# Another order of the three engine queues in the attention part of a graph-layer kernel

## The chip, the cores and the metric

The kernel runs on one core of one Trainium2 chip. The metric is the device time of one execution in microseconds; the number given for a kernel is the median of its runs. Five engines work side by side, each through its own queue in the order in which its instructions were issued: TensorE (PE in the profile; PEld are its weight loads), VectorE (DVE), ScalarE (ACT), GpSimd (POOL) and SyncE (SP), which issues most of the transfers.

## The reference

A chain of four pre-normed layers on x (512 nodes by 512 features), with 16384 edges. Only the first, an attention layer, is touched by the change:

```python
h = jnp.maximum(_layernorm(x, axis=-1), 0.0)
q = (h @ Wq + bq).reshape(N, H, HEAD)        # 8 heads of 64
k = (h @ Wk + bk).reshape(N, H, HEAD)
v = (h @ Wv + bv).reshape(N, H, HEAD)
scores = jnp.einsum('nhd,mhd->nhm', q, k) / np.sqrt(HEAD)
adj = jnp.zeros((N, N)).at[src, dst].set(1.0)
scores = jnp.where(adj[:, None, :] == 0, -1000000000.0, scores)
attn = jax.nn.softmax(scores, axis=1)        # over the heads
attn_out = jnp.einsum('nhm,mhd->nhd', attn, v).reshape(N, D_OUT) @ Wo + bo
h1 = _layer_norm(h + attn_out, g1, be1)
ff = jax.nn.relu(h1 @ W1 + b1) @ W2 + b2
x = x + _layer_norm(h1 + ff, g2, be2)
```

After it come a neighbour mean, a mixture of four graph experts and a graph convolution, each after its own norm and ReLU of x. They use the matrix of edge counts (C and its transpose CT in the code), its row sums (cnt, pdeg) and their reciprocals.

## The kernel before, in words

The work has four stages in time. Up to about 51 us the edge counts are summed in PSUM by one-hot products (`count`, L279), with the first projections between them. From 51 to 138 us the softmax part runs. Up to 191 us follow the output projection and the feed-forward layer of the attention block. All after it, the other three layers, is the same in both kernels.

The softmax part goes over eight blocks i of 256 by 128 scores for eight heads: the columns' half hf = i // 4 (LEFT or RIGHT) and the row block b = i % 4. For each block, in this chain:

- `scores(i)` (L310, PE): eight small products into one tile psc of four PSUM banks. There is one such tile, so the next block's scores wait until this one is read for the last time.
- `copies(i)` (L321, ACT): the scores as bf16. `maximum(i)` (L326 to 328, DVE): three steps down to the maximum over the heads. `maximum_far(i)` (L334, DVE): adds a large number where there is no edge.
- `minus_max(i)`: on PE as a product (L348), or for i of 0, 5 and 7 on DVE (L344). `exponent(i)` (L354, ACT).
- off that chain: `total(i)` (L363 to 366, DVE) the sum, `logs(i)` (L373, 374, ACT) and `weight(i)` (L380, 381, DVE) its reciprocal, `spread(i)` (L386, DVE) the scaling, `gather(i)` (L396, PE) the product with v into aps, `squares(i)` (L357, ACT) a check value.

Between these steps lie others: `v_mm` and `v_add` (L403, L407) make v, `project_mm` and `project_out` (L201, L243) the right half of q, `digits` (L502 to 510, DVE) and the call that it returns, `dg[b]()` (L511, ACT) make the counts CT, `add_bo` (L410, DVE) adds a bias to h.

The part after it: `heads_out` (L414, ACT) moves aps into qT; `wo_mm` (L418, PE) is the output projection; `residual` (L422, DVE), `stats_begin`, `stats_end` and `norm1` are the first norm; `turn1` (L439, PE) and `turn1_out` (L444, ACT) transpose it; `ff_up_mm` (L201 into pff, PE) and `ff_up_out` (L465, ACT) the first feed-forward product in four pairs f = 0, 2, 4, 6 per half; `ff_down` (L474, PE) the second, one product pd per row block; `affine1` (L449, 450) and `add_be2` (L492) are DVE steps that prepare the residuals; `norm2_a` (L480), `norm2_b` (L485, and statistics of the new x) and `norm2_c` (L185, ACT, the scaled h) are the second norm and the next layer's first. `turn(hT, h, b, "h2_")` (L196 PE, L197 ACT) transposes that h. `count_turn(b)` (L428, PE) transposes the counts, and the call that it returns, `ct[b]()` (L429, ACT), writes C. `score_check`, `check_mm` (L520, PE: a product of one row, pall) and `check_out` (L525, DVE) make one flag. `pdeg` is a product with ones that sums C, and the lines from L804 on its reciprocals and others, on DVE.

With `ff_down(3)` the part ends. Its residual on DVE (y23), the norms of row block 3 and its transpose must be done before the next layer's sums of hT (`ws_hT`, L866) and with them the product pbe_b (L900).

What sets the order: the block is written under a manual schedule of PE, DVE and ACT. Each engine executes its instructions in the order in which the calls stand in the source, and waits at each for its inputs and for its output buffer. PSUM tiles come from small pools: `banks[:] = [(ps_mm, "mm")]` names the pool that the next `bank()` draws from. ps_mm has two buffers and ps_x four; ps_x takes the room of psc, once the last block is through. Weight loads are issued by SP in their own order, each once the last reader of the buffer that it takes is done:

```python
wpool = ctx.enter_context(tc.tile_pool(name="wpool", bufs=5))
ps_mm = tc.alloc_tile_pool(name="ps_mm", bufs=2, space=PSUM)
ps_sc = tc.alloc_tile_pool(name="ps_sc", bufs=1, space=PSUM)
```

Of the kernel before, what the change touches and what calls it, by code (L numbers as in the profile page):

```python
# [27 lines left out]
FB = FF // P  # L28
# [10 lines left out]
def fast(  # L39
# [4 lines left out]
    nc = tc.nc  # L44
# [279 lines left out]
    def maximum(i):  # L324
        a, b = high[i]
        nc.vector.tensor_tensor(a, a, b, op=ALU.max)  # L326
        nc.vector.tensor_tensor(a[:, 0:2, :], a[:, 0:2, :], a[:, 2:4, :], op=ALU.max)
        nc.vector.tensor_tensor(a[:, 0, :], a[:, 0, :], a[:, 1, :], op=ALU.max)
        high[i] = a[:, 0, :]

    def maximum_far(i):
        hf, b, cols = place(i)
        far[i] = soft.tile([P, W], R, tag="mr", name=f"mr{i}")
        nc.vector.tensor_add(far[i], high[i], none[:, b, cols])  # L334
# [117 lines left out]
    ffT = {}  # L452

    def ff_up_mm(hf, f):

        if f == 0:
            ffT[hf] = ffp.tile([P, FB, W], F32, tag="ffT", name=f"ffT{hf}")
        p = bank(f"pff{hf}_{f}").rearrange("p (i n) -> p i n", i=2)
        for i in range(2):
            mm(p[:, i, :], [(blk(w1[f // 4], k, (f + i) % 4), hT[:, k, hf * W:(hf + 1) * W]) for k in range(KB)])  # L460
        return p
# [67 lines left out]
    with tc.manual_schedule(engines={ET.PE, ET.DVE, ET.Activation}):  # L529
# [58 lines left out]
        vi = soft.tile([P, M], I32, tag="vi", bufs=1, name="vi")  # L588
        banks[:] = [(ps_mm, "mm")]
        pj, pv, dg, ct, pw, ys, st, rs, tp, pu, pd, y2, a2, n1 = ({} for _ in range(14))  # L590
        maximum(0)
        pv[0] = v_mm(0)
        nc.vector.tensor_copy(vi, cps)
        dg[0] = digits(0)
        maximum_far(0)
        minus_max(0)
        v_add(0, pv[0])
        squares(0)
        dg[1] = digits(1)
        exponent(0)  # L600
        scores(1)
        total(0)
        copies(1)
        maximum(1)
        maximum_far(1)
        dg[0]()
        add_bo(2)
        dg[3] = digits(3)
        dg[2] = digits(2)
        logs(0)  # L610
        pv[1] = v_mm(1)
        v_add(1, pv[1])
        minus_max(1)
        exponent(1)
        pj[2] = project_mm(wq, BQ, 2, RIGHT)
        weight(0)
        scores(2)
        spread(0)
        squares(1)
        project_out(pj[2], qT, BQ, 2, RIGHT)  # L620
        copies(2)
        pj[0] = project_mm(wq, BQ, 0, RIGHT)
        maximum(2)
        maximum_far(2)
        pj[1] = project_mm(wq, BQ, 1, RIGHT)
        total(1)
# [7 lines left out]
        project_out(pj[0], qT, BQ, 0, RIGHT)
        project_out(pj[1], qT, BQ, 1, RIGHT)
        scores(3)
        logs(1)
        weight(1)
        pj[3] = project_mm(wq, BQ, 3, RIGHT)
        copies(3)  # L640
        spread(1)
        maximum(3)
        maximum_far(3)
        pv[2] = v_mm(2)
        minus_max(3)
        logs(2)
        gather(1)
        project_out(pj[3], qT, BQ, 3, RIGHT)
        squares(3)
        weight(2)  # L650
        exponent(3)
        add_bo(0)
        dg[2]()
        dg[1]()
        spread(2)
        v_add(2, pv[2])
        total(3)
        scores(4)
        copies(4)
        pv[3] = v_mm(3)  # L660
        maximum(4)
        logs(3)
        maximum_far(4)
        squares(4)
        add_bo(1)
        v_add(3, pv[3])
        weight(3)
        minus_max(4)
        exponent(4)
        gather(2)  # L670
        scores(5)
        spread(3)
        total(4)
        copies(5)
        gather(3)
        maximum(5)
        ct[1] = count_turn(1)
        heads_out(0)
        maximum_far(5)
        pw[0] = bank("pwo0")  # L680
        wo_mm(0, pw[0], range(KB))
        logs(4)
        minus_max(5)
        squares(5)
        weight(4)
        ct[1]()
        scores(6)
        copies(6)
        pw[1] = bank("pwo1")
        wo_mm(1, pw[1], range(KB))  # L690
        spread(4)
        ys[0] = residual(pw[0], 0, "y")
        st[0] = stats_begin([ys[0]], "l1_0")
        exponent(5)
        ct[0] = count_turn(0)
        maximum(6)
        rs[0] = stats_end(st[0])
        ct[0]()
        ys[1] = residual(pw[1], 1, "y")
        st[1] = stats_begin([ys[1]], "l1_1")  # L700
        maximum_far(6)
        norm1(0, ys[0], *rs[0])
        rs[1] = stats_end(st[1])
        norm1(1, ys[1], *rs[1])
        squares(6)
        gather(4)
        minus_max(6)
        tp[0] = turn1(0)
        total(5)
        exponent(6)  # L710
        turn1_out(0, tp[0])
        scores(7)
        logs(5)
        pu[0, 0] = ff_up_mm(0, 0)
        total(6)
        copies(7)
        pu[0, 2] = ff_up_mm(0, 2)
        ff_up_out(0, 0, pu[0, 0])
        weight(5)
        maximum(7)  # L720
        maximum_far(7)
        logs(6)
        minus_max(7)
        spread(5)
        pu[0, 4] = ff_up_mm(0, 4)
        exponent(7)
        gather(5)
        total(7)
        logs(7)
        weight(6)  # L730
        spread(6)
        ps_sc.release()
        ps_x = tc.alloc_tile_pool(name="ps_x", bufs=4, space=PSUM, reuse_waits="tile")
        banks[:] = [(ps_x, "x")]
        pu[0, 6] = ff_up_mm(0, 6)
        weight(7)
        gather(6)
        spread(7)
        nc.vector.tensor_add(be1_b, be1_b, b2_b)
        affine1(1)  # L740
        gather(7)
        squares(7)
        banks[:] = [(ps_mm, "mm")]
        score_check()
        pall = check_mm()
        check_out(pall)
        ff_up_out(0, 4, pu[0, 4])
        heads_out(1)
        ff_up_out(0, 2, pu[0, 2])
        banks[:] = [(ps_x, "x")]  # L750
        pw[3] = bank("pwo3")
        wo_mm(3, pw[3], range(KB))
        add_be2(1)
        pw[2] = bank("pwo2")
        wo_mm(2, pw[2], range(KB))
        ff_up_out(0, 6, pu[0, 6])
        ys[3] = residual(pw[3], 3, "y")
        st[3] = stats_begin([ys[3]], "l1_3")
        rs[3] = stats_end(st[3])
        norm1(3, ys[3], *rs[3])  # L760
        ys[2] = residual(pw[2], 2, "y")
        st[2] = stats_begin([ys[2]], "l1_2")
        affine1(0)
        rs[2] = stats_end(st[2])
        add_be2(0)
        norm1(2, ys[2], *rs[2])
        pd[1] = bank("pf21")
        ff_down(1, pd[1], range(FB))
        y2[1] = residual(pd[1], 1, "y2")
        banks[:] = [(ps_mm, "mm")]  # L770
        tp[1] = turn1(1)
        turn1_out(1, tp[1])
        a2[1] = norm2_a(1, y2[1])
        affine1(2)
        banks[:] = [(ps_x, "x")]
        pd[0] = bank("pf20")
        ff_down(0, pd[0], range(FB))
        pu[1, 4] = ff_up_mm(1, 4)
        banks[:] = [(ps_mm, "mm")]
        ct[2] = count_turn(2)  # L780
        n1[1] = norm2_b(1, *a2[1])
        affine1(3)
        norm2_c(1, n1[1])
        y2[0] = residual(pd[0], 0, "y2")
        a2[0] = norm2_a(0, y2[0])
        banks[:] = [(ps_x, "x")]
        pu[1, 6] = ff_up_mm(1, 6)
        pu[1, 2] = ff_up_mm(1, 2)
        pu[1, 0] = ff_up_mm(1, 0)
        ff_up_out(1, 4, pu[1, 4])  # L790
        n1[0] = norm2_b(0, *a2[0])
        ff_up_out(1, 2, pu[1, 2])
        banks[:] = [(ps_mm, "mm")]
        ct[3] = count_turn(3)
        add_be2(3)
        ff_up_out(1, 6, pu[1, 6])
        add_be2(2)
        ct[2]()
        ff_up_out(1, 0, pu[1, 0])
        norm2_c(0, n1[0])  # L800
        ct[3]()
# [4 lines left out]
        nc.vector.reciprocal(ideg_b, ideg_b)
        ideg = const.tile([P, NB], F32, name="ideg")
        icnt = const.tile([P, NB], F32, name="icnt")
# [9 lines left out]
        nc.vector.reciprocal(icnt, icnt)  # L818
        nc.vector.reciprocal(nanf, cnt)
        nc.vector.tensor_scalar(nanf, nanf, 0.0, None, op0=ALU.mult)  # L820
        banks[:] = [(ps_mm, "mm")]
        turn(hT, h, 0, "h2_")
        turn(hT, h, 1, "h2_")
        banks[:] = [(ps_x, "x")]
        p2, p3 = bank("pf22"), bank("pf23")
        ff_down(2, p2, range(FB))
        y = residual(p2, 2, "y2")
        n1 = norm2_b(2, *norm2_a(2, y))
        norm2_c(2, n1)
        ff_down(3, p3, range(FB))  # L830
        y23 = residual(p3, 3, "y2")
# [875 lines left out]
```

## Time and profile before

| | us |
|---|---|
| median of 3 runs | 500.74 (498.92 to 501.13) |
| time of the profiled execution | 498.76 |
| span of the profiled execution | 496.9 |
| mean granted TensorE clock in it | 0.997 |
| TensorE busy, 51 to 116 us (65.00) | 59.15 |
| TensorE busy, 116 to 138 us (22.00) | 21.83 |
| TensorE busy, 138 to 191 us (53.00) | 51.67 |
| TensorE busy, 191 to 203 us (12.00) | 11.60 |
| TensorE busy, 203 to 230 us (27.00) | 26.25 |

How to read it: times within the profile count from the start of its span. A row of the timeline has the start, the time, the engine, the line, the operation, output and inputs, and in brackets how long the engine had been idle before it and what ended that. A row of the chain has start, time and what; the chain is followed back from the last instruction, at each step to what released it. A row of the waits has the total, the number and the longest wait. Matmul rows include the end of the pipeline, so that the next can start a little before one ends. Busy TensorE is not TensorE at its peak.

### The profile page before, as it was taken

Reading aid. Unit: us, or ns where it says so; the run is one execution under the profiler, and the core shown is the slowest. Engines: PE = TensorE matmul, PEld = TensorE weight load, DVE = VectorE, ACT = ScalarE, POOL = GpSimd, SP = SyncE. Lnnn points to the kernel's source line nnn. Section 1 sums busy time; section 2 is a strip of 40 time slices with the busy share of each in tenths; the row PEclk is TensorE's granted clock in tenths of the full one; section 3 lists DMA queues with packets and bytes.
Section 4 is the critical chain, followed back from the end, with each engine's and each line's share of the span. In section 5 each row is a group of like instructions: output and inputs, shape, how many; then the busy total and the mean of one; then the engine's idle time right before and its main releaser. Section 6 shows DMA issues by size and latency. Waiting matters only on the chain.

```text
span 496.9 us, 5670 instructions
## 1 busy us (share of the span) xinstructions
PE 470.6 (95%) x2140; PEld 355.2 (71%) x2140; DVE 347.5 (70%) x752; ACT 173.1 (35%) x352; POOL 2.8 (1%) x10
## 2 busy tenths in 40 slices
PE   2999899998999989999999999999999999999995
PEld 1888465547745845677888888888888888885643
DVE  8998989899968457889857169713784147646842
ACT  3899557657222322216011121203102111122443
POOL 2000000000000000000000000000000000000000
PEclk9999999999999999999999999999999999999998
DMA  7820202300031325050004042204121040000002
GB/s 265 288 95 1 85 1 84 128 0 2 0 92 43 121 86 190 0 168 3 1 0 169 7 163 86 84 1 160 22 89 69 1 169 1 1 1 0 0 1 90
DMA packets 18498, 34.42 MB, mean 69 GB/s; under 512 B 1528, under 2 KB 2080, under 8 KB 18464
## 3 DMA queue, kind: packets, MB, share of 16 engines
q1 hardware_dynamic: 17504, 32.47, 19.3%
q10 hardware_dynamic: 960, 1.51, 0.9%
q8 instruction: 19, 0.31, 0.2%
q14 instruction: 15, 0.12, 0.1%
HBM read 32.93 MB, written 1.05 MB: 68 GB/s over the span
## 4 chain that ended last, share of the span: by engine, by line
PE 76%; DVE 15%; ACT 6%; issue 2%; DMA 0%; DVEq 0%; ACTq 0%
PE pe_b L900 8%; PE pq L201 6%; PE pe_a L900 6%; PE pf L474 6%; PE pe_c L900 5%; PE pqk L201 4%; PE pz_b L900 4%; PE po_b L900 3%; PE ph L201 3%; PE pff L201 3%; PE pal L201 3%; PE po L201 3%; PE cps L279 3%; PE pz_c L900 2%; PE po_c L900 2%; PE pz_a L900 2%
## 5 line engine op out<-in xcount | busy, mean ns | idle before, releaser
L906 DVE TENSOR_TENSOR u_sum<-pe_b,u_first 128x512 f32<-128x512 f32 x12 | 8.3, 690 | 48.8 <-PE pe_b L900 48.8
L201 PE MATMUL pq<-zz,C 128*128 128x512 f32 x128 | 32.6, 408 | 0.0
L1161 ACT ACTIVATE re<-te,gt 128x512 f32<-128x512 f32 x16 | 11.6, 723 | 55.9 <-DVE te L1159 55.9
L277 DVE TENSOR_SCALAR ohs<-iota_h,src_f,dw_i 128x256 bf16<-128x256 f16 x102 | 28.0, 342 | 2.4 <-PE cps L279 2.4
L1123 ACT ACTIVATE eT<-u_sum,vecs 128x256 f32<-128x256 f32 x24 | 10.9, 500 | 50.9 <-DVE u_sum L906 50.9
L201 PE MATMUL pff<-hT,w 128*128 128x256 f32 x128 | 28.5, 381 | 0.0
L201 PEld LDWEIGHTS pq<-zz,C 128*128 128x128 f32 x128 | 23.9, 188 | 6.4 <-issue 1.0
L474 PE MATMUL pf<-w,ffT 128*128 128x512 f32 x64 | 28.0, 592 | 0.0
L201 PEld LDWEIGHTS pff<-hT,w 128*128 128x128 f32 x128 | 24.1, 190 | 4.3 <-issue 0.6
L279 PE MATMUL cps<-ohs,ohd 128*128 128x256 bf16 x102 | 17.5, 281 | 9.6 <-DVE ohs L277 9.6
L279 PEld LDWEIGHTS <-ohd 128*128 128x128 f16 x128 | 15.2, 145 | 11.3 <-DVE ohd L268 8.5
L474 PEld LDWEIGHTS pf<-w,ffT 128*128 128x128 f32 x64 | 12.0, 190 | 14.3 <-issue 14.3
L843 ACT CAST zz<-u_sum 128x512 fp32r<-128x512 f32 x12 | 7.4, 618 | 37.7 <-DVE u_sum L906 37.7
L310 PE MATMUL psc<-qT,kT 64*128 64x256 f32 x128 | 16.0, 389 | 3.1 <-ACT s L354 1.7
L321 ACT CAST m<-psc 128x1024 bf16<-128x1024 f32 x16 | 15.4, 1014 | 9.8 <-PE psc L310 9.8
L386 DVE SCALAR_TENSOR_TENSOR s<-s,r 128x2048 f32<-128x2048 f32 x8 | 18.3, 2290 | 0.2
L310 PEld LDWEIGHTS psc<-qT,kT 64*128 64x128 f32 x128 | 12.0, 186 | 7.6 <-ACT s L354 3.7
L906 DVE TENSOR_TENSOR u_sum<-pz_b,u_first 128x512 f32<-128x512 f32 x12 | 8.3, 690 | 11.9 <-PE pz_b L900 11.6
L900 PE MATMUL pe_b<-sums,wr 128*128 128x256 f32 x64 | 16.4, 379 | 0.0
L900 PE MATMUL pe_b<-sums,wl 128*128 128x256 f32 x64 | 16.4, 379 | 0.0
L1162 DVE TENSOR_TENSOR xs<-xs,re 128x512 f32<-128x512 f32 x16 | 11.0, 690 | 7.6 <-ACT re L1161 7.6
L201 PE MATMUL pqk<-hT,wk 128*128 128x256 f32 x64 | 15.2, 381 | 0.9 <-ACT hT L197 0.9
(312 smaller groups left out, 1056.3 us busy)
## 6 DMA issues: line engine op xcount, KB each, us to landing
wr<-in_L_gnn_Wr_dram SPq DMA_DIRECT2D x8, 1024.0 KB, 5.1
wl<-in_L_gnn_Wl_dram SPq DMA_DIRECT2D x8, 1024.0 KB
w<-in_L_gnn_W_dram SPq DMA_DIRECT2D x5, 1024.0 KB, 10.6
wq<-in_L_gnn_Wq_dram ACTq DMA_DIRECT2D x1, 1024.0 KB
wk<-in_L_gnn_Wk_dram SPq DMA_DIRECT2D x1, 1024.0 KB
wv<-in_L_gnn_Wv_dram SPq DMA_DIRECT2D x1, 1024.0 KB, 5.2
wo<-in_L_gnn_Wo_dram SPq DMA_DIRECT2D x1, 1024.0 KB
bl_b<-in_L_gnn_bl_dram SPq DMA_DIRECT2D x4, 256.0 KB, 3.2
```

The source lines that it names most:

```text
L201: nc.tensor.matmul(p, a, c, start=(i == 0), stop=(i == len(pairs) - 1))
L277: nc.vector.tensor_scalar(ohs, iota_h, src_f[:, c:c + 1], dw_f[:, c:c + 1], op0=ALU.is_equal, op1=ALU.mult)
L279: nc.tensor.matmul(cps, ohd[0][:, :, c % 8], ohs, start=(c == 0), stop=(c == NCH - 1))
L310: nc.tensor.matmul(psc[i][:, 4 * g + j, :], kT[o:o + HD, j, b * P:(b + 1) * P], qT[o:o + HD, j, cols], start=(j % 2 == 0), stop=True, skip ...
L321: nc.scalar.copy(t[k].rearrange("p (g j) n -> p g j n", g=2), p[:, :, 2 * k:2 * k + 2, :])
L386: nc.vector.scalar_tensor_tensor(s, s, LEAST, rz[i].to_broadcast([P, H, W]), op0=ALU.max, op1=ALU.mult)
L474: nc.tensor.matmul(p, ffT[b // 2][:, f, c:c + P], w2[f // 4][:, f % 4, :], start=(f == 0), stop=(f == FB - 1))
L900: nc.tensor.matmul(p[:, m, :], l[i][:, k, m * P:(m + 1) * P], r[i][:, k, :], start=fresh, stop=(k == 1), skip_group_check=True)
L906: nc.vector.tensor_add(t, p, x)
L1123: nc.scalar.activation(eT[:, 2 * i + m, j * W:(j + 1) * W], v[:, m, :], AF.Relu, bias=vecs[:, o:o + 1])
L1161: nc.scalar.activation(r, t, AF.Relu, scale=gt[:, b, e:e + 1])
L1162: nc.vector.tensor_add(xs[:, b, :], xs[:, b, :], r)
```

## The change

The change puts the calls from `ohp.release()` to the third down product into another order. The calls themselves are the same, with the same shapes, and so are the kernel before and after this stretch. Three further points go with it: the tile ffT is now made at whichever pair f comes first, since the pairs come in the order 6, 2, 0, 4; the pair that is drawn from ps_x first is now f = 0; and the fourth down product gets its bank on its own. The diff, cut to the moves that the text speaks of:

```diff
-        if f == 0:
+        if hf not in ffT:
             ffT[hf] = ffp.tile([P, FB, W], F32, tag="ffT", name=f"ffT{hf}")
...
+        pv[0] = v_mm(0)
+        add_bo(1)
         maximum(0)
-        pv[0] = v_mm(0)
         nc.vector.tensor_copy(vi, cps)
...
+        total(1)
         pj[0] = project_mm(wq, BQ, 0, RIGHT)
         maximum(2)
+        project_out(pj[1], qT, BQ, 1, RIGHT)
+        logs(1)
         maximum_far(2)
-        pj[1] = project_mm(wq, BQ, 1, RIGHT)
-        total(1)
+        spread(0)
+        project_out(pj[0], qT, BQ, 0, RIGHT)
+        weight(1)
         minus_max(2)
-        add_bo(3)
+        exponent(2)
+        pj[3] = project_mm(wq, BQ, 3, RIGHT)
+        dg[2]()
+        scores(3)
         dg[3]()
-        gather(0)
-        exponent(2)
+        pv[2] = v_mm(2)
+        project_out(pj[3], qT, BQ, 3, RIGHT)
+        spread(1)
         total(2)
         squares(2)
...
         copies(3)
-        spread(1)
         maximum(3)
+        gather(0)
+        logs(2)
         maximum_far(3)
-        pv[2] = v_mm(2)
         minus_max(3)
...
         scores(5)
-        spread(3)
-        total(4)
         copies(5)
+        dg[1]()
         gather(3)
-        maximum(5)
         ct[1] = count_turn(1)
         heads_out(0)
-        maximum_far(5)
+        total(4)
         pw[0] = bank("pwo0")
         wo_mm(0, pw[0], range(KB))
+        maximum(5)
         logs(4)
+        maximum_far(5)
+        ct[1]()
         minus_max(5)
...
         rs[0] = stats_end(st[0])
-        ct[0]()
+        ct[0] = count_turn(0)
+        maximum_far(6)
+        squares(6)
         ys[1] = residual(pw[1], 1, "y")
         st[1] = stats_begin([ys[1]], "l1_1")
-        maximum_far(6)
         norm1(0, ys[0], *rs[0])
+        minus_max(6)
+        ct[0]()
         rs[1] = stats_end(st[1])
+        exponent(6)
+        gather(4)
         norm1(1, ys[1], *rs[1])
-        squares(6)
-        gather(4)
-        minus_max(6)
         tp[0] = turn1(0)
-        total(5)
-        exponent(6)
         turn1_out(0, tp[0])
         scores(7)
+        total(5)
+        total(6)
+        nc.vector.tensor_add(be1_b, be1_b, b2_b)
+        copies(7)
         logs(5)
-        pu[0, 0] = ff_up_mm(0, 0)
-        total(6)
-        copies(7)
+        maximum(7)
+        weight(5)
+        pu[0, 6] = ff_up_mm(0, 6)
+        maximum_far(7)
+        minus_max(7)
+        exponent(7)
         pu[0, 2] = ff_up_mm(0, 2)
...
+        banks[:] = [(ps_mm, "mm")]
+        ct[2] = count_turn(2)
+        affine1(0)
         squares(7)
-        banks[:] = [(ps_mm, "mm")]
+        ct[3] = count_turn(3)
+        add_be2(0)
+        heads_out(1)
         score_check()
         pall = check_mm()
         check_out(pall)
         ff_up_out(0, 4, pu[0, 4])
-        heads_out(1)
-        ff_up_out(0, 2, pu[0, 2])
+        ff_up_out(0, 0, pu[0, 0])
+        affine1(1)
+        ct[3]()
         banks[:] = [(ps_x, "x")]
         pw[3] = bank("pwo3")
         wo_mm(3, pw[3], range(KB))
...
         pd[0] = bank("pf20")
         ff_down(0, pd[0], range(FB))
+        turn1_out(1, tp[1])
+        a2[1] = norm2_a(1, y2[1])
+        y2[0] = residual(pd[0], 0, "y2")
         n1[1] = norm2_b(1, *a2[1])
         pu[1, 6] = ff_up_mm(1, 6)
         pu[1, 2] = ff_up_mm(1, 2)
+        ff_up_out(1, 6, pu[1, 6])
+        a2[0] = norm2_a(0, y2[0])
+        ff_up_out(1, 2, pu[1, 2])
+        n1[0] = norm2_b(0, *a2[0])
+        norm2_c(1, n1[1])
+        affine1(3)
+        affine1(2)
+        norm2_c(0, n1[0])
+        add_be2(2)
+        pu[1, 4] = ff_up_mm(1, 4)
+        ff_up_out(1, 4, pu[1, 4])
         pu[1, 0] = ff_up_mm(1, 0)
+        ff_up_out(1, 0, pu[1, 0])
...
         nc.vector.tensor_scalar(ideg_b, pdeg, 1.0, None, op0=ALU.max)
         banks[:] = [(ps_x, "x")]
+        turn(hT, h, 1, "h2_")
+        add_be2(3)
+        pd[2] = bank("pf22")
+        ff_down(2, pd[2], range(FB))
+        y2[2] = residual(pd[2], 2, "y2")
+        turn(hT, h, 0, "h2_")
+        a2[2] = norm2_a(2, y2[2])
+        banks[:] = [(ps_mm, "mm")]
         nc.vector.reciprocal(ideg_b, ideg_b)
...
         nc.vector.tensor_scalar(nanf, nanf, 0.0, None, op0=ALU.mult)
-        banks[:] = [(ps_mm, "mm")]
-        turn(hT, h, 0, "h2_")
-        turn(hT, h, 1, "h2_")
         banks[:] = [(ps_x, "x")]
-        p2, p3 = bank("pf22"), bank("pf23")
-        ff_down(2, p2, range(FB))
-        y = residual(p2, 2, "y2")
-        n1 = norm2_b(2, *norm2_a(2, y))
+        p3 = bank("pf23")
+        n1 = norm2_b(2, *a2[2])
         norm2_c(2, n1)
         ff_down(3, p3, range(FB))
         y23 = residual(p3, 3, "y2")
```

Two of these orders don't show in the cut: on ACT, the built queue has heads_out(1), then the two pairs of ffT writes for f = 4 and f = 0, then ct[3](), and the product pall waits for ct[3]() because the two buffers of ps_mm are held by the count turns 2 and 3.

More of the change, by code (lines that the diff above doesn't have):

```diff
@@ L595, in fast @@
         maximum_far(0)
+        squares(0)
         minus_max(0)
         v_add(0, pv[0])
-        squares(0)
+        scores(1)
+        exponent(0)
+        copies(1)
         dg[1] = digits(1)
-        exponent(0)
-        scores(1)
         total(0)
-        copies(1)
         maximum(1)
         maximum_far(1)
-        dg[0]()
-        add_bo(2)
+        pv[1] = v_mm(1)
+        logs(0)
+        minus_max(1)
         dg[3] = digits(3)
+        exponent(1)
+        v_add(1, pv[1])
         dg[2] = digits(2)
[L610 to L614, printed above, removed]
         pj[2] = project_mm(wq, BQ, 2, RIGHT)
@@ L617, in fast @@
         scores(2)
-        spread(0)
+        add_bo(0)
         squares(1)
@@ L621, in fast @@
         copies(2)
+        pj[1] = project_mm(wq, BQ, 1, RIGHT)
+        total(1)
         pj[0] = project_mm(wq, BQ, 0, RIGHT)
         maximum(2)
+        project_out(pj[1], qT, BQ, 1, RIGHT)
+        logs(1)
         maximum_far(2)
-        pj[1] = project_mm(wq, BQ, 1, RIGHT)
-        total(1)
+        spread(0)
+        project_out(pj[0], qT, BQ, 0, RIGHT)
+        weight(1)
         minus_max(2)
-        add_bo(3)
+        exponent(2)
+        pj[3] = project_mm(wq, BQ, 3, RIGHT)
+        dg[2]()
+        scores(3)
         dg[3]()
-        gather(0)
-        exponent(2)
+        pv[2] = v_mm(2)
+        project_out(pj[3], qT, BQ, 3, RIGHT)
+        spread(1)
         total(2)
         squares(2)
[L634 to L639, printed above, removed]
         copies(3)
-        spread(1)
         maximum(3)
+        gather(0)
+        logs(2)
         maximum_far(3)
-        pv[2] = v_mm(2)
         minus_max(3)
-        logs(2)
+        exponent(3)
         gather(1)
-        project_out(pj[3], qT, BQ, 3, RIGHT)
         squares(3)
         weight(2)
[L651 to L654, printed above, removed]
+        add_bo(2)
+        v_add(2, pv[2])
         spread(2)
-        v_add(2, pv[2])
         total(3)
         scores(4)
+        pv[3] = v_mm(3)
         copies(4)
-        pv[3] = v_mm(3)
+        logs(3)
         maximum(4)
-        logs(3)
         maximum_far(4)
-        squares(4)
-        add_bo(1)
-        v_add(3, pv[3])
+        add_bo(3)
         weight(3)
@@ L669, in fast @@
         exponent(4)
+        v_add(3, pv[3])
+        dg[0]()
+        squares(4)
+        spread(3)
         gather(2)
         scores(5)
-        spread(3)
-        total(4)
         copies(5)
+        dg[1]()
         gather(3)
-        maximum(5)
         ct[1] = count_turn(1)
         heads_out(0)
-        maximum_far(5)
+        total(4)
         pw[0] = bank("pwo0")
         wo_mm(0, pw[0], range(KB))
+        maximum(5)
         logs(4)
+        maximum_far(5)
+        ct[1]()
         minus_max(5)
+        scores(6)
+        weight(4)
         squares(5)
-        weight(4)
-        ct[1]()
-        scores(6)
+        spread(4)
         copies(6)
@@ L690, in fast @@
         wo_mm(1, pw[1], range(KB))
-        spread(4)
         ys[0] = residual(pw[0], 0, "y")
@@ L694, in fast @@
         exponent(5)
-        ct[0] = count_turn(0)
         maximum(6)
         rs[0] = stats_end(st[0])
-        ct[0]()
+        ct[0] = count_turn(0)
+        maximum_far(6)
+        squares(6)
         ys[1] = residual(pw[1], 1, "y")
         st[1] = stats_begin([ys[1]], "l1_1")
-        maximum_far(6)
         norm1(0, ys[0], *rs[0])
+        minus_max(6)
+        ct[0]()
         rs[1] = stats_end(st[1])
+        exponent(6)
+        gather(4)
         norm1(1, ys[1], *rs[1])
-        squares(6)
-        gather(4)
-        minus_max(6)
         tp[0] = turn1(0)
-        total(5)
-        exponent(6)
         turn1_out(0, tp[0])
         scores(7)
+        total(5)
+        total(6)
+        nc.vector.tensor_add(be1_b, be1_b, b2_b)
+        copies(7)
         logs(5)
-        pu[0, 0] = ff_up_mm(0, 0)
-        total(6)
-        copies(7)
-        pu[0, 2] = ff_up_mm(0, 2)
[L718 to L731, printed above, removed]
+        maximum(7)
[4 more added lines that the diff above has]
+        exponent(7)
+        pu[0, 2] = ff_up_mm(0, 2)
         ps_sc.release()
         ps_x = tc.alloc_tile_pool(name="ps_x", bufs=4, space=PSUM, reuse_waits="tile")
+        spread(5)
+        total(7)
         banks[:] = [(ps_x, "x")]
-        pu[0, 6] = ff_up_mm(0, 6)
+        pu[0, 0] = ff_up_mm(0, 0)
+        logs(6)
+        weight(6)
+        ff_up_out(0, 6, pu[0, 6])
+        gather(5)
+        pu[0, 4] = ff_up_mm(0, 4)
+        spread(6)
+        gather(6)
+        logs(7)
+        ff_up_out(0, 2, pu[0, 2])
         weight(7)
-        gather(6)
         spread(7)
-        nc.vector.tensor_add(be1_b, be1_b, b2_b)
-        affine1(1)
         gather(7)
+        banks[:] = [(ps_mm, "mm")]
+        ct[2] = count_turn(2)
+        affine1(0)
         squares(7)
-        banks[:] = [(ps_mm, "mm")]
+        ct[3] = count_turn(3)
+        add_be2(0)
+        heads_out(1)
         score_check()
@@ L752, in fast @@
         wo_mm(3, pw[3], range(KB))
-        add_be2(1)
         pw[2] = bank("pwo2")
         wo_mm(2, pw[2], range(KB))
-        ff_up_out(0, 6, pu[0, 6])
         ys[3] = residual(pw[3], 3, "y")
@@ L759, in fast @@
         rs[3] = stats_end(st[3])
+        ct[2]()
         norm1(3, ys[3], *rs[3])
@@ L762, in fast @@
         st[2] = stats_begin([ys[2]], "l1_2")
[L763 to L766, printed above, removed]
         pd[1] = bank("pf21")
         ff_down(1, pd[1], range(FB))
+        add_be2(1)
+        rs[2] = stats_end(st[2])
+        norm1(2, ys[2], *rs[2])
         y2[1] = residual(pd[1], 1, "y2")
@@ L771, in fast @@
         tp[1] = turn1(1)
-        turn1_out(1, tp[1])
-        a2[1] = norm2_a(1, y2[1])
-        affine1(2)
         banks[:] = [(ps_x, "x")]
@@ L777, in fast @@
         ff_down(0, pd[0], range(FB))
-        pu[1, 4] = ff_up_mm(1, 4)
-        banks[:] = [(ps_mm, "mm")]
-        ct[2] = count_turn(2)
+        turn1_out(1, tp[1])
+        a2[1] = norm2_a(1, y2[1])
+        y2[0] = residual(pd[0], 0, "y2")
         n1[1] = norm2_b(1, *a2[1])
[L782 to L786, printed above, removed]
         pu[1, 6] = ff_up_mm(1, 6)
         pu[1, 2] = ff_up_mm(1, 2)
+        ff_up_out(1, 6, pu[1, 6])
[9 more added lines that the diff above has]
+        ff_up_out(1, 4, pu[1, 4])
         pu[1, 0] = ff_up_mm(1, 0)
-        ff_up_out(1, 4, pu[1, 4])
-        n1[0] = norm2_b(0, *a2[0])
-        ff_up_out(1, 2, pu[1, 2])
+        ff_up_out(1, 0, pu[1, 0])
         banks[:] = [(ps_mm, "mm")]
[L794 to L801, printed above, removed]
         pdeg = bank("pdeg")
@@ L820, in fast @@
         nc.vector.tensor_scalar(nanf, nanf, 0.0, None, op0=ALU.mult)
-        banks[:] = [(ps_mm, "mm")]
-        turn(hT, h, 0, "h2_")
-        turn(hT, h, 1, "h2_")
         banks[:] = [(ps_x, "x")]
-        p2, p3 = bank("pf22"), bank("pf23")
-        ff_down(2, p2, range(FB))
-        y = residual(p2, 2, "y2")
-        n1 = norm2_b(2, *norm2_a(2, y))
+        p3 = bank("pf23")
+        n1 = norm2_b(2, *a2[2])
         norm2_c(2, n1)
```

## The prediction, made before the changed kernel ran

> **What bounds the kernel now.** I read the page first, then the chain that ended last in order of time, then the waits of TensorE between 50 and 205 us, then the timeline there engine by engine. The page's busy row makes TensorE the engine to watch:
>
> ```profile
> PE 470.6 (95%) x2140; PEld 355.2 (71%) x2140; DVE 347.5 (70%) x752; ACT 173.1 (35%) x352; POOL 2.8 (1%) x10
> ```
>
> But 95% is a mean. From 54 to 132 us the chain goes round PE, ACT and DVE, once per block of scores:
>
> ```profile
> 65.41 2.02 PE psc L310 x16
> 67.51 1.94 ACT m L321 x2
> 69.47 0.70 DVE m L326
> 71.55 1.19 PE psc L348 x4
> ```
>
> One round is scores, copy, maximum, minus the maximum, exponent: 74.76 - 65.41 = 9.35 us. The four PSUM banks of the scores are reused, so rounds can't overlap. From 137.68 on the chain is nearly pure TensorE, up to one crossing at 200.9 to 203.1 us, where TensorE waits for DVE again:
>
> ```profile
> 200.90 0.59 ACT hT L197
> ...
> 201.52 0.70 DVE ws_hT L866
> ...
> 203.09 1.10 PE pbe_b L900 x4
> ```
>
> What TensorE waits for in all:
>
> ```profile
> PE psc L310 <- ACT s L354: 1.7, 5, 0.9
> PE psc L348 <- DVE mr L334: 1.7, 4, 0.5
> PE psc L310 <- DVE s L344: 1.3, 2, 1.0
> PE psc L348 <- ACT r_l L143: 1.0, 1, 1.0
> PE pdeg L201 <- ACT C L429: 1.0, 1, 1.0
> ```
>
> And DVE's queue ahead of that crossing, which decides this case:
>
> ```profile
> 176.98 3.35 DVE L806 RECIPROCAL ideg_b<-ideg_b 128x512 f32<-128x512 f32 x1
> ...
> 182.49 0.17 DVE L820 TENSOR_SCALAR nanf<-nanf 128x4 f32<-128x4 f32 x1
> 184.57 0.69 DVE L422 TENSOR_TENSOR y<-pf,h 128x512 f32<-128x512 f32 x1 [1.91 <-PE pf L474]
> ...
> 190.70 0.16 DVE L152 TENSOR_TENSOR rs_n<-nt_n,r_n 128x1 f32<-128x1 f32 x1
> 191.44 0.69 DVE L422 TENSOR_TENSOR y<-pf,h 128x512 f32<-128x512 f32 x1 [0.57 <-PE pf L474]
> ```
>
> The reciprocals run while DVE would otherwise wait for the third down product (1.91 us idle even so). Block 2's norms then just fit under the fourth: 0.57 us to spare.
>
> **The change part by part.** No operation is added or removed; I walk each engine's new order with the durations above. An operation starts at the later of its queue's turn and its last input.
>
> *Softmax rounds, 51 to 116 us.* add_bo(1) (0.60) now precedes maximum(0), which had 0.45 of slack: +0.2. spread(0) and total(1) change places around maximum(2), without effect: rounds 1 and 2 keep 9.35. In round 3 before, spread(1) ended at 80.26 though the copy was done at 78.73: 1.4 us lost. After, DVE reaches maximum(3) at 79.2, its result is out at 81.3; but v_mm(2) and gather(0) now stand before minus_max(3) on TensorE: 76.9 + 3.44 + 1.84 = 82.2 against 82.33. What DVE saves, TensorE's queue takes back. Round 5: dg[1] (0.63) enters ACT before heads_out(0); wo_mm(0) starts about 0.5 later and ends at 103.4, where DVE frees the banks anyway (103.48 before): 0. Round 6: far(6) goes before residual(1), so minus_max(6) starts at 110.7 instead of 112.43; but on ACT ct[0]() (0.6) now lies between block 1's square root and exponent(6), which can start at 113.3 instead of 113.64. Sum: -0.3 at scores(7). Twice a gain of over a microsecond is lost to a neighbour in a queue.
>
> *Last round and gathers, 116 to 138.* copies(7) is put before logs(5) (-0.65), but turn1_out and weight(5), 0.91, stand before far(7): minus_max(7) at 122.3 against 122.04. Two up products fit before it; the third takes a bank that minus_max(7) frees (124.7). Then up, gather, up, two gathers: the last gather ends at 137.45 against 137.31: +0.1.
>
> *Count turns and check.* ct[2] and ct[3] (0.43 each) move ahead of check_mm. With both PSUM buffers of that pool taken, the one-row product pall must wait for ct[3]() on ACT, and the built queues do carry that wait. Ahead of it on ACT stand heads_out(1) (to 138.0), four ffT writes (1.57) and ct[3]() (0.6): 140.15. Queued behind pall on TensorE are wo_mm(3), wo_mm(2), the down products; on DVE, check_out and affine1(1) (cheap, nobody near). TensorE stands from 138.3 to 140.2; wo_mm(3) starts at 140.3 instead of 137.61: +2.7.
>
> *Up to the third down product.* Before, wo_mm(3) to ff_down(2) takes 177.50 - 137.61 = 39.89. Out of it go the two count turns (0.44 + 0.36), the wait of pdeg for C (0.98), the wait of the turn (0.35) and one turn, now behind ff_down(2) (0.49): 37.3. ff_down(2) starts at 177.6 (177.3 if all waits shrink), and y of block 2 at 184.5 against 184.57. So the pall wait is paid back, and up to here the change is worth 0.0. DVE's part here is later too (norm2_b(1) waits behind residual(0), which waits for the down product until 162.1), but h of block 1 is ready at 172, its turn comes at 176.9; the last ffT write ends at 177.1, with 0.3 of cover.
>
> *The tail.* Now DVE's queue after y of block 2 is: its statistics and t (184.57 to 186.97: 2.40), then the reciprocal and twelve small operations (176.98 to about 182.6: 5.6), then norm2_b and norm2_c (186.97 to 190.86: 3.9). Sum 11.9, under a fourth down product of 6.87. Residual(3) starts at 184.5 + 11.9 = 196.4, not 191.44: +5.0. In before the 5.6 were hidden by waiting; that cover is gone. From there to pbe_b before: 203.09 - 191.44 = 11.65. Two collisions on ACT vanish, since u_first (193.16) and hT (197.03) held lv back: 0.3 and 0.7. 10.65 remain: pbe_b at 207.05. **+4.0 us.**
>
> One rule speaks against this idle time, the clock gate's. Trainium skill, "TensorE: Matmul & The Clock Gate", Part 1: after an idle window of about 3.4 us TensorE runs at half clock until it has been busy for one. The trace's PEclk row shows 9 in every slice but the last, with waits of 1.0 us at most from 50 us on, so no row tests it. Here TensorE stands about 2.5 us before the turn of block 3 and 1.1 before pbe_b. By the row: no cost. By the rule, if a window counted as idle: 3.4 us of products at half speed, an estimate of +1.7. I take 0 and keep 1.7 for the range.
>
> *Transfers.* wns waits for pu[1,4] instead of pu[1,6]: issued near 173 instead of 167.40; with the 10.6 us of the like-sized w load it lands by 184, and pbe_a needs it at 191.5. wr follows at 176, needed on DVE past 212. The other loads move little or earlier. Cost 0; if wns's cover were gone, each us late would delay pbe_a by one, of which TensorE's wait behind DVE hides three. POOL has nothing here.
>
> *After pbe_b* the orders are the same and TensorE is busy 26.25 of 27 us up to 230, so the shift goes through to the end. Profiled: span 496.9, time 498.76; 498.76 + 4.0 = 502.8. The median shown is 500.74, 2.0 above this execution; so 500.74 + 4.0 = 504.7.
>
> **Rivals.**
> 1. *The softmax part really gets shorter.* Ideal rounds are five of 9.35 and one of 8.60 (round 5, freed by DVE): 55.35 against 115.63 - 56.13 = 59.5 before. At best 4.1 us are won; all pass to ff_down(2), since that part is TensorE in order: 504.7 - 4.1 = 500.6, no change. For it: 1.4 and 1.7 us of DVE delay really go. Against: gather(0) before minus_max(3), ct[0]() before exponent(6). It decides from 1.5 us on (below +2.5, "same"); 501.8 at half of the best.
> 2. *The pall wait is not paid back*, because ACT is later or pdeg still waits: up to 2 more, 506.7. For it: the walk has only 0.3 of cover at the last ffT write.
> 3. *The clock drops*: 506.4.
> 4. *The tail doesn't bind*: were the reciprocals hidden, 500.7. The built order speaks against it: residual(3) stands behind all of them on DVE, and nothing passes on that queue in the trace (maximum(3) stood ready at 78.73 and started after spread(1)).
>
> **How the numbers follow.** A measurement of this kernel can tell about 0.5%, 2.5 us, from no change. My forecast, +3 to +5: 0.55. Rival 1: 0.22, a fifth of it (with an early tail's luck) faster. Rivals 2 and 3: 0.20. Rival 4: 0.03. Faster 0.05, same 0.18, slower 0.77. The range takes rival 1 at half its best and rivals 2 and 3: 501.8 to 506.8.
>
> **What would show it.** In the changed profile: pall waiting about 1.9 us for ACT C; y of block 2 near 184.5; RECIPROCAL after it; residual(3) near 196.4 with no idle time before it; pbe_b waiting for DVE or h at 207. It is wrong if scores(7) starts before 114, if wo_mm(3) starts before 139, or if residual(3) is released by TensorE.

## The result and the profile after

The changed kernel takes 503.92 us (median of 8 runs, 502.05 to 505.40), the kernel before 499.24 us beside it (8 runs): ratio 1.0076, 95% interval 1.0057 to 1.0095. By the ratio it is slower by about 3.8 us; the prediction had +4.0, and 504.7 with a range of 501.8 to 506.8. The executions of one kernel fall into two groups some 2 us apart, so that a median of eight depends on how many of each it caught: the two medians lie 4.7 us apart, and the ratio, which is taken over all runs and is not their quotient, is the figure to use.

The profiled execution took 504.62 us with a span of 502.8. That is 5.9 us over the profile of before, and 2.07 of them are there before the change begins: v_mm(0), its first product, starts at 53.59 instead of 51.52. The first projections, which are the same in both kernels, take one of two times from execution to execution. In the timeline of TensorE, before:

```profile
13.89 1.99 PE L201 MATMUL pqk<-hT,wk 128*128 128x256 f32 x8 [0.87 <-ACT hT L197]
```

and after:

```profile
14.26 3.77 PE L201 MATMUL pqk<-hT,wk 128*128 128x256 f32 x8 [0.62 <-ACT hT L197]
```

The same eight products take 3.77 us instead of 1.99. This lies ahead of the change, and it moves all that follows. So what is compared below is counted from the start of v_mm(0). TensorE has it in the kernel before at

```profile
51.52 3.60 PE L403 MATMUL pv<-wv,hT 128*128 128x512 f32 x8
```

and in the changed kernel, with two later rows that matter, at

```profile
53.59 3.60 PE L403 MATMUL pv<-wv,hT 128*128 128x512 f32 x8
...
142.04 0.19 PE L520 MATMUL pall<-deg,ones 128*1 128x6 f32 x2 [1.71 <-ACT C L429]
...
208.64 2.10 PE L900 MATMUL pbe_b<-ws_wns,ws_hT 128*128 128x256 f32 x8
```

Now the answers to the lines of before. The page's busy row of the changed kernel gives TensorE no less to do, only a longer span to do it in:

```profile
PE 474.4 (94%) x2140; PEld 357.3 (71%) x2140; DVE 347.0 (69%) x752; ACT 173.2 (34%) x352; POOL 2.8 (1%) x10
```

What TensorE waits for between 50 and 215 us (total, number, longest):

```profile
PE tp_h L196 <- ACT h L185: 2.4, 2, 2.1
PE psc L348 <- DVE mr L334: 2.4, 4, 0.9
PE pall L520 <- ACT C L429: 1.7, 1, 1.7
```

Two waits of over a microsecond are new: pall for the counts that ACT writes, and the turn of block 3 for h (2.1). The wait of pdeg for C (1.0) and that of minus_max for r_l (1.0) are gone; other short waits of the softmax rounds came and went.

And DVE's queue in the tail, from its timeline:

```profile
186.06 0.69 DVE L422 TENSOR_TENSOR y<-pf,h 128x512 f32<-128x512 f32 x1 [6.08 <-PE pf L474]
188.46 3.34 DVE L811 RECIPROCAL ideg_b<-ideg_b 128x512 f32<-128x512 f32 x1
...
193.96 0.17 DVE L825 TENSOR_SCALAR nanf<-nanf 128x4 f32<-128x4 f32 x1
197.84 0.68 DVE L422 TENSOR_TENSOR y<-pf,h 128x512 f32<-128x512 f32 x1
```

Before y of block 2, DVE stands idle for 6.08 us. Behind it the reciprocal begins, and residual(3), the last row, has no bracket: it is no longer released by TensorE but by DVE's own queue. In the chain that ended last of the changed kernel the reciprocal now appears by name, where before the chain was TensorE alone from the third down product to the turn of block 3:

```profile
179.95 6.02 PE pf L474 x14
186.06 0.70 DVE y L422
...
188.54 3.26 DVE ideg_b L811
...
197.92 0.61 DVE y L422
```

Where the time went, in stretches between starts that the timelines of the profiles give (us):

| kernel | v_mm(0) to scores(7) | to first wo_mm behind the gathers | to y of block 2 | y2 to y3 | y3 to pbe_b | pbe_b to the end |
|---|---|---|---|---|---|---|
| before | 64.11 | 21.98 | 46.96 | 6.87 | 11.65 | 293.81 |
| after | 63.63 | 24.94 | 43.90 | 11.78 | 10.80 | 294.16 |

The first three stretches together give 133.05 before and 132.47 after: the long way up to the third down product is 0.6 us shorter, and the tail from there to pbe_b is 4.1 us longer.

### The profile page after: what moved, and what is told of

Read it like the earlier page. It is cut to its first block, busy times and chain, and to the rows that moved or that the text cites. A ratio compares the mean times of both kernels' runs of the same rounds, so it can differ in the third digit from the quotient of the medians.

```text
span 502.8 us, 5671 instructions
## 1 busy us (share of the span) xinstructions
PE 474.4 (94%) x2140; PEld 357.3 (71%) x2140; DVE 347.0 (69%) x752; ACT 173.2 (34%) x352; POOL 2.8 (1%) x10
## 4 chain that ended last, share of the span: by engine, by line
PE 76%; DVE 15%; ACT 5%; issue 1%; DMA 1%; SPq 0%; DVEq 0%; ACTq 0%
PE pe_b L900 8%; PE pq L201 6%; PE pe_a L900 6%; PE pe_c L900 5%; PE pff L201 4%; PE pqk L201 4%; PE pf L474 4%; PE pz_b L900 4%; PE po_b L900 3%; PE ph L201 3%; PE po L201 3%; PE psc L310 2%; PE cps L279 2%; PE pz_c L900 2%; PE po_c L900 2%; PE po_a L900 2%
## 5 line engine op out<-in xcount | busy, mean ns | idle before, releaser
L279 PEld LDWEIGHTS <-ohd 128*128 128x128 f16 x128 | 15.3, 145 | 11.9 <-DVE ohd L268 8.8
L474 PEld LDWEIGHTS pf<-w,ffT 128*128 128x128 f32 x64 | 11.9, 190 | 13.9 <-issue 13.9
L201 PE MATMUL pqk<-hT,wk 128*128 128x256 f32 x64 | 17.0, 414 | 0.6 <-ACT hT L197 0.6
L310 PEld LDWEIGHTS psc<-qT,kT 64*128 64x128 f32 x128 | 11.9, 186 | 7.0 <-ACT s L354 3.3
L906 DVE TENSOR_TENSOR u_sum<-pz_b,u_first 128x512 f32<-128x512 f32 x12 | 8.3, 689 | 11.9 <-PE pz_b L900 11.6
```

Source lines behind the costliest of these rows:

```text
L201: nc.tensor.matmul(p, a, c, start=(i == 0), stop=(i == len(pairs) - 1))
L279: nc.tensor.matmul(cps, ohd[0][:, :, c % 8], ohs, start=(c == 0), stop=(c == NCH - 1))
L310: nc.tensor.matmul(psc[i][:, 4 * g + j, :], kT[o:o + HD, j, b * P:(b + 1) * P], qT[o:o + HD, j, cols], start=(j % 2 == 0), stop=True, skip ...
L474: nc.tensor.matmul(p, ffT[b // 2][:, f, c:c + P], w2[f // 4][:, f % 4, :], start=(f == 0), stop=(f == FB - 1))
L906: nc.vector.tensor_add(t, p, x)
```

## The experiments

The theory: the reciprocal and the small operations behind it stand on DVE's critical path in the tail (some 4 us), and the reordered softmax part is worth nothing on balance, since the wait of pall takes away what the rest gives. The rival: the tail has room, and the wait of pall or the clock costs the time. Ratios are to the kernel before, run on the same chip; its median beside the first seven kernels is 500.57 us, beside the last 498.89, so the ratios are what to compare, not the times. As above, a ratio is taken over all runs and need not be the quotient of two medians.

### The reciprocal back ahead of y of block 2

```diff
+        nc.vector.reciprocal(ideg_b, ideg_b)
...
         y2[2] = residual(pd[2], 2, "y2")
         turn(hT, h, 0, "h2_")
         a2[2] = norm2_a(2, y2[2])
-        banks[:] = [(ps_mm, "mm")]
-        nc.vector.reciprocal(ideg_b, ideg_b)
...
```

The small operations behind the reciprocal, up to nanf, move with it.

> The changed kernel, with the reciprocal and the small operations behind it put back ahead of residual(2) on DVE, where the profile of the changed kernel has 6.1 us of idle DVE; turn(0) of h keeps its new place behind residual(2). Theory (DVE's queue in the tail decides): residual(3) is released by TensorE again, about 4.5 us earlier, the two collisions on ACT come back (1.0), pbe_b about 3.5 us earlier: near 500.4, within 0.5% of the kernel before. Rival (the softmax part and the wait of pall cost the time): 503 to 504, as the changed kernel.

Measured: 499.84 us, ratio 1.0002 (0.9984 to 1.0021). From v_mm(0) to pbe_b it takes 151.27 us, against 155.05 in the changed kernel: 3.8 us less. DVE's timeline of this kernel:

```profile
177.89 3.35 DVE L807 RECIPROCAL ideg_b<-ideg_b 128x512 f32<-128x512 f32 x1
...
183.99 0.69 DVE L422 TENSOR_TENSOR y<-pf,h 128x512 f32<-128x512 f32 x1 [0.44 <-PE pf L474]
...
191.29 0.69 DVE L422 TENSOR_TENSOR y<-pf,h 128x512 f32<-128x512 f32 x1 [1.02 <-PE pf L474]
```

The same operations now fill the idle time, and both residuals are released by TensorE again. What is left of the change, the whole order up to the third down product, makes no difference that can be measured.

### The reciprocal late, in the kernel before

```diff
-        nc.vector.reciprocal(ideg_b, ideg_b)
...
         y = residual(p2, 2, "y2")
-        n1 = norm2_b(2, *norm2_a(2, y))
+        a22 = norm2_a(2, y)
+        nc.vector.reciprocal(ideg_b, ideg_b)
...
+        n1 = norm2_b(2, *a22)
```

> The kernel before, with only the reciprocal and the small operations behind it moved, to between norm2_a and norm2_b of block 2, nothing else changed. Theory (they are 5.6 us of DVE time with no cover there): 3.5 to 4 us slower than the kernel before, ratio about 1.0075. Rival (the tail has room for them): ratio 1.000.

Measured: 503.16 us, ratio 1.0075 (1.0048 to 1.0103). This one move, in the old order, costs what the whole change costs. pbe_b comes 3.7 us later (155.30 against 151.57 after v_mm(0)), with y2 to y3 at 11.77 us, as in the changed kernel (11.78). (The medians alone, 6 runs against 51, would give 1.0052; the stretches of the profile agree with the ratio.) DVE's timeline has the reciprocal behind y of block 2, and residual(3) without a wait for TensorE:

```profile
184.56 0.69 DVE L422 TENSOR_TENSOR y<-pf,h 128x512 f32<-128x512 f32 x1 [7.62 <-PE pf L474]
186.96 3.34 DVE L814 RECIPROCAL ideg_b<-ideg_b 128x512 f32<-128x512 f32 x1
...
196.33 0.68 DVE L422 TENSOR_TENSOR y<-pf,h 128x512 f32<-128x512 f32 x1
```

### The one-row product ahead of the count turns

```diff
+        squares(7)
+        score_check()
+        pall = check_mm()
+        check_out(pall)
         ct[2] = count_turn(2)
         affine1(0)
-        squares(7)
         ct[3] = count_turn(3)
         add_be2(0)
         heads_out(1)
-        score_check()
-        pall = check_mm()
-        check_out(pall)
```

> The changed kernel, with squares(7), score_check, check_mm and check_out put ahead of count_turn(2) and count_turn(3) on every engine, so that pall no longer waits for ct[3]() on ACT. Theory (TensorE works in order from there to the third down product, so every microsecond of its wait counts): 1.7 us less than the changed kernel, about 502.2, y of block 2 earlier by as much. Rival (the freed time is lost again to the wait of pdeg for C and to the turns, as these took 1.8 us in the kernel before): no difference from the changed kernel, 503.9.

Measured: 501.85 us, ratio 1.0031 (1.0018 to 1.0045), some 2.2 us less than the changed kernel. In its timeline of TensorE pall has lost its wait, and the turns run straight on:

```profile
134.21 3.67 PE L396 MATMUL aps<-s,v 128*64 128x256 f32 x32
137.81 0.19 PE L520 MATMUL pall<-deg,ones 128*1 128x6 f32 x2
137.94 1.09 PE L428 MATMUL pc<-ident,CT 128*128 128x128 f32 x8
138.87 7.03 PE L418 MATMUL pwo<-wo,qT 128*128 128x512 f32 x16
```

y of block 2 comes 1.98 us earlier after v_mm(0), which starts at 52.17 here (130.49 against 132.47):

```profile
182.66 0.69 DVE L422 TENSOR_TENSOR y<-pf,h 128x512 f32<-128x512 f32 x1 [6.09 <-PE pf L474]
```

So all of it is kept and none is lost to a later wait. Two microseconds were bought with a tiny product's place in a queue.

### Both edits

> Both of these edits in the changed kernel: the reciprocal early in the tail, and pall ahead of the count turns. If the two costs are separate and add: 3.5 + 1.7 = 5.2 us less than the changed kernel, about 498.7, 0.5 to 1 us below the kernel before. If the earlier third down product takes away the idle DVE time that hides the reciprocal, or if the 1.7 us are lost to later waits: 500 to 500.5, as with the early reciprocal alone.

Measured: 498.48 us, ratio 0.9961 (0.9946 to 0.9976). From v_mm(0) to pbe_b: 149.30 us, 5.75 less than the changed kernel, where the two edits alone gave 3.78 and 2.38. The two costs are separate. That 3.78 and 2.38 give more than 5.75 comes from TensorE's clock, which was low for a while in the profile of the changed kernel (see the kernel in which TensorE is kept busy: 154.67 us at full clock). Against that kernel the edits give 3.40, 2.00 and together 5.37 us, and so they add. With both gone, the new order beats the kernel before by 2 us.

### Two exchanges in the softmax rounds

To the kernel with both edits:

```diff
         maximum(3)
-        gather(0)
         logs(2)
         maximum_far(3)
         minus_max(3)
+        gather(0)
         exponent(3)
...
-        ct[0]()
         rs[1] = stats_end(st[1])
         exponent(6)
+        ct[0]()
```

> The kernel with both edits (reciprocal early, pall first), and in its softmax part two more exchanges: gather(0) behind minus_max(3) on TensorE, and ct[0]() behind exponent(6) on ACT. Theory (these two neighbours in a queue took back what the searched order saved on DVE): minus_max(3) starts about 1.0 us earlier, as its input is ready at 81.03 and TensorE takes it at 82.27; exponent(6) about 0.6 earlier; together 1.0 to 1.6 us at scores(7) and at the end, about 497 where the kernel with both edits has 498.5. Rival (another wait, of the exponents or of maximum, ends the rounds there anyway): no difference.

Measured: 500.06 us, ratio 0.9988 (0.9972 to 1.0005): by the ratios 1.3 us *more* than with both edits alone, which neither theory expected (the two ran on different chips, and their intervals just overlap; the profiles decide). minus_max(3) does come 1.08 us earlier after v_mm(0) (29.67 against 30.75). But scores(4) comes 0.79 later (34.76 against 33.97), and scores(7) 1.59 later (65.24 against 63.65): the first exchange costs 0.79 us in round 3, the second 0.80 in round 6. ACT's timeline, at exponent(3):

```profile
86.66 1.94 ACT L354 ACTIVATE s<-psc 128x1024 f32<-128x1024 f32 x2 [4.26 <-PE aps L396]
```

and TensorE's, at turn1(0):

```profile
118.32 0.87 PE L439 MATMUL tp_h<-ident,h 128*128 128x128 f32 x6 [1.10 <-ACT C L429]
```

exponent(3) waits for gather(0): the tile s has three buffers in the code, and the fourth tile takes the one that gather(0) reads. turn1 needs both PSUM buffers of its pool, and one holds the counts until ct[0]() has read them. So these two neighbours were not in the way by chance; each frees a buffer that the very next step takes. A fourth buffer for s was not tried.

### The reciprocal three times

```diff
         nc.vector.reciprocal(ideg_b, ideg_b)
+        nc.vector.reciprocal(ideg_b, ideg_b)
+        nc.vector.reciprocal(ideg_b, ideg_b)
```

> The changed kernel with the 128x512 RECIPROCAL made three times in place instead of once, which puts 1/deg again where the first left it. Theory (behind y of block 2 the DVE queue has no slack at all until pbe_b): 2 x 3.34 = 6.7 us more than the changed kernel, in full, about 510.6; TensorE's wait before the turn of block 3 grows from 2.1 to about 8.8 us, so the half clock behind it may add some. Rival (DVE is not what ends last in the tail): less than 3 us.

Measured: 510.77 us, ratio 1.0202 (1.0178 to 1.0226): 6.3 us over the changed kernel's ratio. y2 to y3 grows from 11.78 to 18.55 us, by 6.77, which is twice 3.38. There is no slack at all behind y of block 2. From TensorE's timeline:

```profile
205.66 1.11 PE L196 MATMUL tp_h<-ident,h 128*128 128x128 f32 x4 [7.09 <-ACT h L185]
206.57 5.16 PE L201 MATMUL pal<-wcs,hT 128*128 128x512 f32 x8
```

After 7.09 us without work, a turn takes 1.11 us instead of 0.66 and the next product 5.16 instead of 3.60, at a granted clock of 0.50 from 203 to 209 us. These 2.0 us of TensorE lie entirely under DVE's work here: y3 to pbe_b is 10.39 us, less than in the changed kernel.

### TensorE kept busy before the turn of block 3

```diff
-    def alpha_mm(b):
+    def alpha_mm(b, twice=0):
         p = bank(f"pal{b}")
+        if twice:
+            mm(p, [(blk(hT, k, b), wcs[:, k, :]) for k in range(twice)])
...
-        al.append(alpha_mm(1))
+        al.append(alpha_mm(1, 2))
```

> The changed kernel, with the first half of alpha_mm(1)'s products made twice (the second time over the first, so the sums stay), which fills 1.8 of the 2.1 us for which TensorE waits before the turn of block 3. Theory (the idle time there leads to half clock in the products behind it, in some executions): the second group of pbe_a takes 1.9 us and not 3.4, the mean clock is 0.998 in all runs where half of the changed kernel's have 0.993, and the time is 0 to 0.8 us less. Rival (the low clock has another cause): 0.993 remains in about half of the runs. If the added products themselves were on the path: up to 1.8 us more.

Measured: 504.00 us, ratio 1.0070 (1.0047 to 1.0092), no difference from the changed kernel. In its profile the products after the turn run at full rate; TensorE's timeline:

```profile
205.09 0.66 PE L196 MATMUL tp_h<-ident,h 128*128 128x128 f32 x4 [0.40 <-ACT h L185]
205.58 1.89 PE L900 MATMUL pbe_a<-wns,hT 128*128 128x256 f32 x8
```

and the same place in the changed kernel:

```profile
204.93 0.66 PE L196 MATMUL tp_h<-ident,h 128*128 128x128 f32 x4 [2.11 <-ACT h L185]
205.43 3.42 PE L900 MATMUL pbe_a<-wns,hT 128*128 128x256 f32 x8
```

That looks like proof, but is not. One of its 6 runs still has a clock of 0.993, against 4 of 8. And the kernel with pall first keeps the wait of 2.11 us, has 1.89 us for the same group in its profile, and a clock of 0.993 or less in only 4 of 22 runs. The kernel before with the reciprocal late has the same wait of 2.11 us, too, 3.05 us for the group, and a clock of 0.993 or 0.994 in all of its 6 runs. So the idle time doesn't decide alone; what else does was not settled. The cost in the profiles is small: y3 to pbe_b is 10.39 us here and 10.80 in the changed kernel, 0.4 us.

### Round 3 ordered within its buffers

To the kernel with both edits:

```diff
         scores(3)
         dg[3]()
-        pv[2] = v_mm(2)
+        gather(0)
         project_out(pj[3], qT, BQ, 3, RIGHT)
...
         squares(2)
+        gather(1)
+        pv[2] = v_mm(2, ks=range(1))
         copies(3)
         maximum(3)
-        gather(0)
...
         exponent(3)
-        gather(1)
+        v_mm(2, pv[2], range(1, KB))
...
-        v_add(2, pv[2])
         spread(2)
+        v_add(2, pv[2])
```

> The kernel with both edits (reciprocal early, pall first), and in round 3 another order that keeps gather(0) ahead of exponent(3): on TensorE gather(0), gather(1) and a quarter of v_mm(2) stand before minus_max(3), the other three quarters behind it; v_add(2) goes behind spread(2) on DVE. Theory (exponent(3) writes the buffer that gather(0) reads, so gather(0) may not stand behind it, and round 3 is bound by TensorE's own 1.93 + 3.44 + 1.1 + 3.68 = 10.15 us): minus_max(3) starts about 1 us earlier than with both edits alone, exponent(3) follows it at once, and scores(4) comes no more than 0.5 us earlier, since the products that are left fill TensorE; the median falls by 0 to 0.5 us. Rival (only the place of gather(0) counted): the rounds get 1 us shorter.

Measured: 496.50 us, ratio 0.9952 (0.9924 to 0.9980), the fastest version here, though its interval overlaps that of the kernel with both edits (0.9961). The profile resolves it better; TensorE's timeline:

```profile
83.75 1.23 PE L348 MATMUL psc<-mr,minus_r 128*128 128x512 f32 x4
84.82 2.73 PE L403 MATMUL pv<-wv,hT 128*128 128x512 f32 x6
87.48 2.00 PE L310 MATMUL psc<-qT,kT 64*128 64x256 f32 x16
```

minus_max(3) comes 1.08 us earlier after v_mm(0) than with both edits alone (29.67 against 30.75), and exponent(3) follows at once. But scores(4) is only 0.57 us earlier (33.40 against 33.97), without a bracket: TensorE's own products fill the round, about as expected (no more than 0.5). scores(7) and pbe_b keep the 0.57 us.

The later kernels in the stretches of the first table (us):

| kernel | to scores(7) | to wo_mm | to y2 | y2 to y3 | y3 to pbe_b |
|---|---|---|---|---|---|
| reciprocal early | 63.63 | 24.94 | 43.83 | 7.30 | 11.57 |
| before, reciprocal late | 64.10 | 21.99 | 46.96 | 11.77 | 10.48 |
| pall first | 63.63 | 23.07 | 43.79 | 11.79 | 10.39 |
| both | 63.65 | 23.07 | 43.72 | 7.30 | 11.56 |
| round 3 ordered | 63.08 | 23.06 | 43.72 | 7.31 | 11.56 |

Each edit shows in its own column and, beyond 0.2 us, nowhere else, but for y3 to pbe_b. That column gets back the two collisions on ACT when the reciprocal is early (the copies u_first and hT then stand in ACT's queue just where the norm of row block 3 needs it).

## Why the prediction was right, step by step

Times of the changed profile are less 2.07 us here, so that they stand on the scale of before.

- *Softmax rounds*: right. minus_max(3) 82.24 (predicted 82.2), minus_max(6) 110.63 (110.7), exponent(6) 113.16 (113.3), scores(7) 115.15 (115.3): -0.5 instead of -0.3. But one sentence of this step was wrong in its reason. I wrote "Twice a gain of over a microsecond is lost to a neighbour in a queue." The experiment with the two exchanges showed that the neighbours hold buffers which the next step needs; to move them costs more.
- *Last round and gathers*: minus_max(7) 121.90 (122.3), last gather's end 137.22 (137.45); 0.4 and 0.2 early.
- *The wait of pall*: right. The profile has 1.71 us; wo_mm(3) at 140.09 (140.3), +2.5 instead of +2.7.
- *Up to the third down product*: right in kind, short in size. I took 2.6 us out of the 39.9; it was 3.1 (142.16 to 178.92 is 36.76). My sum used the waits as the brackets give them. A bracket counts from the modelled end of the last product, which the next could have overlapped: pdeg took 1.28 us instead of 0.94 + 0.98 + 0.50, so its wait alone cost 1.14 and not 0.98. The starts on TensorE give the rest: the wait of the turn cost 0.51 and not 0.35 (from one turn to the next 0.95 us, where a turn alone takes 0.44), and the 64 up products, no longer parted by a count turn, take 13.63 us instead of 3.45 + 10.36. y of block 2 came at 183.99 (184.5): -0.6, not 0.0. The payback did not depend on the wait of pall, though: with pall first, nearly the same stretch of 43.8 us remains, and the 2 us are won.
- *The tail*: right. y2 to y3 took 11.78 us (11.9). residual(3) starts at 195.77 (196.4) with no idle time before it; the reciprocal early and late in either kernel switches this cost off and on. From y3 to pbe_b it is 11.65 us without the late reciprocal and, at full clock, 10.39 with it (I had 10.65). The collisions on ACT behaved as said: from y3 to the last step of the new x's norm, rs_n, DVE takes 7.12 us before and 6.12 after, 1.0 less; the other 0.26 lies behind that step.
- *The clock*: I took 0 for an idle time of 2.5 us. The rule of the Trainium skill ("TensorE: Matmul & The Clock Gate", Part 1: half clock after an idle window of about 3.4 us) spoke against that, and in this execution TensorE was in fact slowed, after 2.11 us of idle time, which is less than the page's window. From the windows of the changed kernel (the clock is the third column from the end):

```profile
199.00:203.00 4.00, 3.82 (x12) 1.56 (x10) 3.69 (x13) 1.11 (x5) 0.00 (x0) 1.00 0.21 59
203.00:207.00 4.00, 2.07 (x9) 1.77 (x10) 3.65 (x10) 1.63 (x4) 0.00 (x0) 0.83 0.02 6
207.00:212.00 5.00, 5.00 (x20) 4.21 (x19) 3.57 (x7) 0.59 (x1) 0.00 (x0) 0.80 0.00 0
```

  In the 9 us of the last two rows TensorE lacks 1.7 us of full clock (0.17 of 4.00 and 0.20 of 5.00), which is the size that I kept for the range. But it cost only 0.4 us up to pbe_b (10.80 against 10.39), since DVE's work covered the rest. The estimate of +1.7 left out that the slowed products lie beside DVE's work.
- *Transfers*: right. wns is issued at 173.18 (near 173), and pbe_a, which reads it, has no idle time before it.
- *After pbe_b*: 294.16 against 293.81, +0.35 where I had 0. Other kernels here have 293.86 to 294.59 for the same code, so this is within what executions differ.

The sum: pbe_b +3.48 (predicted +4.0), the rest +0.35, together 3.8; the ratio, 0.0076 of 499.24, says the same. That 4.0 and 3.8 lie so close is in part luck: the way up to y of block 2 gave 0.6 that I did not have, and the 0.35 behind pbe_b, which no step explains, makes up for part of it. The tail itself came to +4.06.

The predicted 504.7 stood on a first median of three runs, 500.74. Beside the changed kernel the kernel before ran at 499.24, 1.5 lower, and the medians lie 4.7 apart and not 4.0: -1.5 and +0.7 make the 0.8 between 504.7 and 503.92. Both come from how many executions of each group a median caught (5 of the 8 of before lie below 499.6), not from a step of the sum. The low end of the range does not follow from its reason either: half of 4.1 off 504.7 is 502.65, not 501.8. The measured time lies above both.

The rivals: the softmax part gave 0.5 us of the 4.1 that it could have given, and the wait of pall was paid back. Neither decided, and the clock gave 0.4. That the tail doesn't bind is refuted by the moved and the tripled reciprocal.

## What to carry to other kernels

Before an order is taken over, ask for each long operation that nobody waits for (here a reciprocal of 3.35 us, with the small steps behind it 5.6) in which idle time of its engine it lies, and whether it still lies there afterwards: the same operations were free on one side of y and cost 3.4 to 3.8 us on the other. A tiny operation that draws from a small buffer pool can stop a whole engine; put it ahead of those that hold the buffers. And when a step seems to stand in the way of another, look which buffer it frees before moving it.

## What the runs showed of the hardware beyond that

- The first group of projections takes 1.99 us in some executions and 3.77 in others, with the same program up to there (both values appear among the profiles of this study). The Trainium skill ("TensorE: Matmul & The Clock Gate", Part 1) says that the warm-up runs at half rate and that its length varies from run to run, as its window runs free. The durations agree: in both profiles the turns ahead of this group take 1.06 to 1.09 us, later ones 0.60. The granted clock does not show it: it reads 1.00 there in both. Of 51 runs of the kernel before, 20 lie between 498.5 and 499.7 us and 31 between 500.2 and 501.7, and the ten profiles tie the two together: the five executions with 1.99 us are each in the lower group of their kernel's times, the five with 3.77 or 3.78 in the upper. A profile from one group and one from the other differ by 2 us before any change begins, so stretches have to be counted from the first common point behind it.
- A low granted clock came after an idle time of only 2.11 us in two profiles (0.83 and 0.80 in the rows above for one of them), and did not come after the same 2.11 us in a third (1.00).
- A 128x512 f32 RECIPROCAL takes 3.35 us on DVE, where an addition of the same size takes 0.69.
